# Opening transfers of a two-layer attention kernel: one key-half transfer on another queue, weight loads tied to a block of x, seven warming products

## The chip, the cores and the metric

The kernel runs on one core of a Trainium2 chip. Time is the device time of one execution in microseconds (us). The engines are PE (TensorE, matrix products; PEld is its weight load), DVE (VectorE), ACT (ScalarE), POOL (GpSimd) and SP (SyncE, which here only issues transfers). SP and ACT issue transfers on a queue of their own each (q1 and q10 in the profile), POOL on a third (q0). [...]

## The reference, cut to what matters

x has shape (4, 128, 64, 64): four images of 128 channels and n = 4096 tokens. All is f32.

```
# layer 0: attention over tokens, 64 media channels, no scale, no mask
xf  = x.reshape(b, c, n)
q, k, v = wq @ xf, wk @ xf, wv @ xf            # each (b, 64, n)
att = softmax(einsum('bmi,bmj->bij', k, q))
x   = x + wo @ einsum('bij,bmj->bmi', att, v)

# layer 1: tokens t = x as (b, n, 128)
t = t + causal_attention(layernorm(t), Wq, Wk, Wv)
t = t + ffn(layernorm(t), W, V, gamma, beta)   # W, batch norm over all tokens, then
                                               # y_t = sigmoid(wx_t + y_{t-1} @ V.T)
```

## The kernel before, in words

`kernel` builds two paths. `fast_path` computes the result and a flag; `general_path` follows only if the flag says that an assumption on the number ranges failed. All times here are of the fast path.

**Tiling.** A block is BLK = 512 tokens, an image has NB = 8 blocks and NT = 32 tiles of 128 tokens. `xs` holds all images in SBUF. Image 0 is loaded by SP in eight transfers of 256 KB, in the order of blocks 0, 4, 1, 5, 2, 6, 3, 7 (L424 to L426): the fifth block of x, number 4, is the second one loaded.

**Keys and queries of layer 0.** `cols0(b, m)` (L524) makes two products of 128x512: block m with `wqk` (queries in rows 0 to 63, keys in 64 to 127) and block m + 4 with `wkq` (the other way round). DVE copies the first result to `bt.kr`, ACT the second. The scores need queries and keys on the same partitions, so after each copy a transfer of 128 KB moves half of the rows to the other half of the partitions, into `bt.swap` (L541). The first of these transfers, b = 0, m = 0, h = 0, is read by the first score product. The one for h = 1 is read from query block 4 on (`rows0`, L575).

**Values of layer 0.** `vals0` (L543) makes the value product, ACT copies it, and for image 0 `vals0_by_tokens` (L569) turns it with four transposes.

**The opening.** L420 to L422 load `wqk`, `wkq` and `wv0` in five small transfers on ACT's queue. POOL makes `ident`. L457 to L460 load `wo2` (two halves), `wqT`, `wkT` and `wv1` on POOL's queue, and `load_rest` (L511), called once the side work of image 0 is done, issues four more there: `wf`, `vf`, `gamma`, `beta`. Nothing makes POOL wait before these nine, and all of them are issued within the first 7 us. TensorE first runs twelve 128x128 products of `ident` with itself (L494 to L496), whose results nobody reads; an f32 product appears as two records. Then L1008 sets the order of the first tasks:

```python
for task in parts[0][:2] + parts[1][:1] + parts[0][2:]:
    task()
```

So TensorE makes both key products of m = 0, the value product of m = 0, both key products of m = 1 and the four transposes, and then the loop of L1051 starts with the first `scores` (L883). The scratch results of all these (`misc`, L490) share two PSUM buffers, so each product waits until the result two before it is copied out.

**The loop.** Each step issues the scores of an item (two tiles of keys against one block of queries), then the values of the item two steps earlier, then the sums. One task of `side` or `waiting` is added where one is due: the remaining key and value products of image 0, then `form` (L506, reads `wqT` and `wkT`) and `form_half` (L498, reads `vf`, `beta` and `wf`).

The instructions of one engine are placed by a scheduler at build time, so an engine's order can differ from the order of the text where nothing forbids it: the issue of the first half of `wo2` stands ahead of the last step of `ident` on POOL.

Of the kernel before, what the change touches and what calls it, by code (L numbers as in the profile page):

```python
# [9 lines left out]
F32 = mybir.dt.float32  # L10
# [5 lines left out]
P = 128  # L16
BLK = 512
# [342 lines left out]
def fast_path(  # L360
# [22 lines left out]
    nc = tc.nc  # L383
    B, C, N = x.shape
    M = c_wqT.shape[1]
    assert C == P and M == P // 2 and N % CHUNK == 0
    NT = N // P
    NB = N // BLK
# [9 lines left out]
    const = ctx.enter_context(tc.tile_pool(name="const", bufs=1))  # L398
# [6 lines left out]
    xs = xpool.tile([P, B, N], F32, name="xs")  # L405
# [5 lines left out]
    def load(engine, name, shape, *parts):  # L411
        t = const.tile(shape, F32, name=name)
        for dst, src in parts:
            engine.dma_start(out=dst(t), in_=src)
        return t

    whole = lambda t: t
    lo, hi = (lambda t: t[:, 0:M]), (lambda t: t[:, M:P])
    top, bottom = (lambda t: t[0:M]), (lambda t: t[M:P])
# [29 lines left out]
    wf = const.tile([P, P], F32, name="wf")  # L449
    vf = const.tile([P, P], F32, name="vf")  # L450
# [3 lines left out]
    wfc = const.tile([P, P], F32, name="wfc")  # L454
    gamma = const.tile([P, 1], F32, name="gamma")
    beta = const.tile([P, 1], F32, name="beta")
    wo2 = load(nc.gpsimd, "wo2", [P, P], (top, c_woT), (bottom, c_woT))  # L457
    wqT = load(nc.gpsimd, "wqT", [P, P], (whole, a_wqT))
    wkT = load(nc.gpsimd, "wkT", [P, P], (whole, a_wkT))
    wv1 = load(nc.gpsimd, "wv1", [P, P], (whole, a_wv))  # L460
    good = const.tile([P, 2], F32, name="good")
    g1 = const.tile([P, P], F32, name="g1")
    recs = const.tile([P, 2, B, NT], F32, name="recs")
# [18 lines left out]
    with tc.tile_pool(name="batch", bufs=1) as batch, tc.tile_pool(name="rows", bufs=2) as rowp, tc.tile_pool(  # L482
        name="prob", bufs=4
    ) as prob, tc.tile_pool(name="work", bufs=2) as wk, tc.tile_pool(name="stat", bufs=4) as stat, tc.tile_pool(
        name="ps_s", bufs=2, space=PSUM
    ) as ps_s, tc.tile_pool(name="ps_a", bufs=1, space=PSUM) as ps_a, tc.tile_pool(
        name="ps_m", bufs=2, space=PSUM
    ) as ps_m:

        def misc(name):  # L490
            return ps_m.tile([P, BLK], F32, tag="m", name=name)


        wp = misc("warm_ps")  # L494
        for _ in range(12):
            nc.tensor.matmul(wp[:, :P], lhsT=ident, rhs=ident, start=True, stop=True)  # L496

        def form_half():  # L498
            hp = misc("h_ps")
            nc.tensor.matmul(hp[:, 0:1], lhsT=vf, rhs=point5, start=True, stop=True)  # L500
            nc.vector.tensor_tensor(beta_half, hp[:, 0:1], beta, ALU.add)
            cp = misc("c_ps")
            nc.tensor.matmul(cp[:, :P], lhsT=center, rhs=wf, start=True, stop=True)
            nc.vector.tensor_copy(wfc, cp[:, :P])

        def form():  # L506
            gp = misc("g_ps")
            nc.tensor.matmul(gp[:, :P], lhsT=wqT, rhs=wkT, start=True, stop=True)
            nc.vector.tensor_copy(g1, gp[:, :P])

        def load_rest():  # L511
            for t, src in ((wf, f_wT), (vf, f_vT), (gamma, f_gamma), (beta, f_beta)):
                nc.gpsimd.dma_start(out=t, in_=src)

        class Batch:
            pass
# [7 lines left out]
        def cols0(b, m):  # L524

            bt = bs[b]
            if m == 0:
                bt.kr = batch.tile([P, 2, N // 2], F32, tag="kr", name="kr")  # L530
                bt.swap = batch.tile([P, N // 2], F32, tag="swap", name="swap")
                bt.v = batch.tile([P, NT // 2, 2, M], F32, tag="v", name="v0")
            for h, w in enumerate((wqk, wkq)):
                ps = misc("kr_ps")
                nc.tensor.matmul(ps, lhsT=w, rhs=xs[:, b, ts(m + h * NB // 2, BLK)], start=True, stop=True)
                if h:
                    nc.scalar.copy(bt.kr[:, h, ts(m, BLK)], ps)
                else:
                    nc.vector.tensor_copy(bt.kr[:, h, ts(m, BLK)], ps)
                rows, keys = slice(M - h * M, P - h * M), slice(h * M, h * M + M)  # L540
                nc.sync.dma_start(out=bt.swap[keys, ts(m, BLK)], in_=bt.kr[rows, h, ts(m, BLK)])  # L541

        def vals0(b, m):  # L543

# [379 lines left out]
        def sums(it):  # L924

            if it.first:
                bs[it.b].dsum = wk.tile([P, 2, BLK], F32, tag="dsum", name="dsum")
            it.den = den = bs[it.b].dsum
            if all(n == BLK for _, _, n, _ in it.at):
                flat = den.rearrange("p a b -> p (a b)")  # L930
                if it.first:
                    nc.vector.tensor_copy(flat, it.p)  # L932
                else:
                    nc.vector.tensor_tensor(flat, flat, it.p, ALU.add)  # L934
                return
            for h, (t, q0, n, o) in enumerate(it.at):
                if it.first:
                    if q0:
                        nc.gpsimd.memset(den[:, h, :q0], 0.0)
                    nc.vector.tensor_copy(den[:, h, q0:], it.p[:, o : o + n])  # L940
                else:
                    nc.vector.tensor_tensor(den[:, h, q0:], den[:, h, q0:], it.p[:, o : o + n], ALU.add)  # L942
# [51 lines left out]
        def push(slot, chain):  # L994
            step = next(chain, None)
            if step:
                waiting.append((slot + step[0], step[1], chain))

        def keys(b, m):
            mem = []  # L1000
            return [
                lambda: cols0(b, m),
                lambda: mem.append(vals0(b, m)),
                lambda: b or vals0_by_tokens(b, m, mem[0]),
            ]
# [7 lines left out]
        def rows():  # L1013

            if blocks:
                layer, b, g = blocks.pop(0)
                (rows1 if layer else rows0)(b, g)
                if layer == 0:
                    started.append((b, g))

        def tokens():

            while started:
                b, g = started.pop(0)
                tokens0(b, g)
                if g == 2 and b + 1 < B:

                    nc.gpsimd.tensor_copy(
                        xs[:, b + 1].rearrange("p (k n) -> p k n", n=CHUNK)[:, :, 0], bs[b].agg[:, : N // CHUNK]
                    )  # L1030
                    for k in range(N // CHUNK):
                        nc.sync.dma_start(out=xs[:, b + 1, ts(k, CHUNK)], in_=x[b + 1, :, ts(k, CHUNK)])
# [6 lines left out]
        def begin(s):  # L1039
            nonlocal done  # L1040
            if done < s < len(items):
                done = s
                it = items[s]
                if it.first:
                    bs[it.b].rows = bs[it.b].next.pop(0)
                    if it.layer and it.g == 3 and it.b + 1 < B:
                        for m in range(NB // 2):
                            side.extend(keys(it.b + 1, m))
                scores(it)

        for s in range(len(items) + SKEW + 16):  # L1051
            begin(s)
            if SKEW < s < len(items) - 1 and items[s - SKEW].first and items[s + 1].layer == 0:
                ended = items[s - SKEW - 1]
                if ended.layer == 0 and ended.g not in visits[0]:
                    begin(s + 1)
            if 0 <= s - SKEW < len(items):
                it = items[s - SKEW]
                values(it)
                if it.last:  # L1060
                    rows()
                    tokens()
                    for k, g in enumerate(visits[it.layer].get(it.g, ())):
                        push(s, bs[it.b].leave[g](8 * k))
                    push(s, (finish1 if it.layer else finish0)(it.b, it.g))
            if s < len(items):
                sums(items[s])
            due = [w for w in waiting if w[0] <= s]
            if due:
                w = min(due, key=lambda w: w[0])  # L1070
                waiting.remove(w)
                w[1]()
                push(s, w[2])
            elif side:
                side.pop(0)()
                if not side and items[s].b == 0 and items[s].layer == 0:
                    tokens()
                    load_rest()
                    form_half()
        assert not waiting and not side  # L1080

# [5 lines left out]
    with tc.tile_pool(name="xr", bufs=1) as xrp, tc.tile_pool(name="y", bufs=2) as yp, tc.tile_pool(  # L1087
        name="sums", bufs=3
    ) as sums, tc.tile_pool(
        name="ps_y", bufs=1, space=PSUM  # L1090
# [3 lines left out]
        for b in range(BY_C):  # L1094
            for c in range(Q):
                nc.sync.dma_start(
                    out=xc[ts(c, S), b].rearrange("r (g k) s -> r g (k s)", g=NB),
                    in_=x2c[b, :, :, c].rearrange("g r n -> r g n"),
# [36 lines left out]
        late = xs.rearrange("p b (r h k q) -> p b k r h q", h=HALVES, r=TPB, q=P)  # L1135
# [149 lines left out]
```

## Time and profile before

| What | us |
|---|---|
| median of 3 runs (2053.29 to 2053.88) | 2053.53 |
| the profiled execution | 2054.28 |
| its span, first to last instruction | 2052.6 |
| TensorE busy in it | 2036.8 |
| issues of x on SP's queue, first and last start | 0.82, 6.80 |
| issues of weights on POOL's queue, first and last start | 1.43, 6.36 |
| first issue of a key-half transfer | 9.25 |
| first product of scores | 14.05 |
| product of `form`, first of `form_half` | 37.84, 38.17 |

The granted clock of TensorE was 0.999 over the span. In the profile's lines, `out<-in` gives the tiles that an instruction writes and reads, "x8" the number of instructions merged into the line, and the brackets at the end the idle time before it and what ended that. A line with q after the engine's name (SPq, ACTq, POOLq) is the issue of a transfer, or a wait of that engine's sequencer.

### The profile page before, as it was taken

Reading aid. Unit: us, or ns where it says so; the run is one execution under the profiler, and the core shown is the slowest. Engines: PE = TensorE matmul, PEld = TensorE weight load, DVE = VectorE, ACT = ScalarE, POOL = GpSimd, SP = SyncE. Lnnn points to the kernel's source line nnn. Section 1 sums busy time; section 2 is a strip of 40 time slices with the busy share of each in tenths; the row PEclk is TensorE's granted clock in tenths of the full one; section 3 lists DMA queues with packets and bytes.
Section 4 is the critical chain, followed back from the end, with each engine's and each line's share of the span. In section 5 each row is a group of like instructions: output and inputs, shape, how many; then the busy total and the mean of one; then the engine's idle time right before and its main releaser. Section 6 shows DMA issues by size and latency. Waiting matters only on the chain. (4 is left out here: it accounts for less than half of the span.)

```text
span 2052.6 us, 30794 instructions
## 1 busy us (share of the span) xinstructions
PE 2036.8 (99%) x11646; PEld 907.4 (44%) x11646; DVE 1486.6 (72%) x2862; ACT 989.1 (48%) x1071; POOL 137.5 (7%) x237
## 2 busy tenths in 40 slices
PE   9999999999999999999999999999999999999998
PEld 3643354444333345444433335444433334544456
DVE  4799877555889987555588997654578998765568
ACT  4666632323666653333466663333356665333346
POOL 1000011000000011000000001100000000100004
PEclk9999999999999999999999999999999999999999
DMA  3111021231201112222111001123000110210056
GB/s 88 53 33 27 12 42 37 51 79 37 58 2 23 22 22 42 47 62 67 22 53 22 17 17 42 37 68 82 16 17 2 22 23 12 52 42 21 21 115 225
DMA packets 237869, 89.03 MB, mean 43 GB/s; under 512 B 174752, under 2 KB 219296, under 8 KB 237200
## 3 DMA queue, kind: packets, MB, share of 16 engines
q1 hardware_dynamic: 236704, 86.42, 17.7%
q8 instruction: 93, 1.52, 0.3%
q14 instruction: 64, 0.52, 0.1%
q0 software_dynamic: 288, 0.39, 0.1%
q10 hardware_dynamic: 720, 0.16, 0.0%
HBM read 45.84 MB, written 36.89 MB: 40 GB/s over the span
## 5 line engine op out<-in xcount | busy, mean ns | idle before, releaser
L934 DVE TENSOR_TENSOR dsum<-dsum,p 128x1024 f32<-128x1024 f32 x676 | 826.1, 1222 | 429.6 <-ACT p L910 308.5
L908 ACT ACTIVATE p<-s_ps,nshift 128x1024 f32<-128x1024 f32 x512 | 569.3, 1116 | 318.4 <-PE s_ps L894 310.3
L910 ACT ACTIVATE p<-s_ps 128x1024 f32<-128x1024 f32 (+2 forms) x288 | 274.2, 952 | 609.5 <-PE s_ps L903 607.1
L954 PE MATMUL acc<-p,v 64*64 64x512 f32 x4096 | 543.0, 590 | 0.0
L894 PE MATMUL s_ps<-swap,kr 64*64 64x512 f32 x2048 | 539.0, 591 | 2.1 <-DMA swap<-kr 1.2
L894 PE MATMUL s_ps<-kr 64*64 64x512 f32 x2048 | 525.0, 591 | 0.0
L903 PE MATMUL s_ps<-rows,xhT 128*128 128x512 f32 (+3 forms) x1152 | 502.9, 559 | 0.0
L962 PE MATMUL acc<-p,xh 128*128 128x512 f32 (+3 forms) x1152 | 500.9, 557 | 0.0
L962 PEld LDWEIGHTS acc<-p,xh 128*128 128x128 f32 x1152 | 216.2, 190 | 244.3 <-issue 234.2
L903 PEld LDWEIGHTS s_ps<-rows,xhT 128*128 128x128 f32 x1152 | 214.0, 190 | 243.3 <-issue 203.4
L954 PEld LDWEIGHTS acc<-p,v 64*64 64x64 f32 x4096 | 166.6, 133 | 272.5 <-issue 251.6
L894 PEld LDWEIGHTS s_ps<-swap,kr 64*64 64x64 f32 x2048 | 151.4, 133 | 132.3 <-issue 107.7
L894 PEld LDWEIGHTS s_ps<-kr 64*64 64x64 f32 x2048 | 140.7, 133 | 138.0 <-issue 133.6
L666 POOL TENSOR_TENSOR ln_rstd<-ln_var,mhalf 128x4 f32<-128x4 f32 x64 | 68.2, 1065 | 1099.4 <-DVE ln_var L664 1099.4
L942 DVE TENSOR_TENSOR dsum<-dsum,p 128x256 f32<-128x256 f32 (+1 forms) x120 | 55.4, 497 | 64.3 <-POOL p L914 64.3
L652 DVE SCALAR_TENSOR_TENSOR xs<-o_ps,recs,xs 128x128 f32<-128x128 f32 x256 | 74.4, 341 | 3.1
L682 DVE TENSOR_SCALAR xh<-xs,ln_mv,ln_rstd 128x128 f32<-128x128 f32 x252 | 70.2, 342 | 2.2
L914 POOL TENSOR_SCALAR_AFFINE_SELECT p<-p 128x128 f32<-128x128 f32 x128 | 35.9, 304 | 486.4 <-ACT p L910 473.9
L661 DVE BATCH_NORM_STATS2 ln_st<-xs 128x6 f32<-128x128 f32 x256 | 63.2, 269 | 0.0
L932 DVE COPY dsum<-p 128x1024 f32<-128x1024 f32 x60 | 41.0, 683 | 16.0 <-ACT p L910 10.8
L839 ACT COPY xs<-wx_ps 128x512 f32<-128x512 f32 x31 | 18.1, 585 | 65.6 <-DVE stats L835 63.5
L1158 DVE SCALAR_TENSOR_TENSOR z<-xs,scale,y_ps 128x256 f32<-128x256 f32 x100 | 45.0, 480 | 2.6 <-PE y_ps L1156 1.6
(148 smaller groups left out, 989.6 us busy)
## 6 DMA issues: line engine op xcount, KB each, us to landing
xs<-in_xT SPq DMA_DIRECT2D x32, 256.0 KB, 3.0
by_r<-sqT SPq DMA_DIRECT2D x128, 64.0 KB, 2.2
xhT<-by_r SPq DMA_DIRECT2D x128, 64.0 KB, 2.0
by_c<-sqT SPq DMA_DIRECT2D x124, 64.0 KB, 1.8
xhT<-by_c SPq DMA_DIRECT2D x31, 256.0 KB, 2.7
xs<-in_x SPq DMA_DIRECT2D x12, 512.0 KB, 5.9
swap<-kr SPq DMA_DIRECT2D x32, 128.0 KB, 2.3
x2c<-sqT SPq DMA_DIRECT2D x64, 64.0 KB, 2.4
```

What stands on the lines that cost most here:

```text
L652: nc.vector.scalar_tensor_tensor(t, in0=op[:, ts(j, P)], scalar=rec[:, j : j + 1], in1=t, op0=ALU.mult, op1=ALU.add)
L661: nc.vector.bn_stats(st[:, j], xs[:, b, ds(g * BLK + j * P, P)])
L666: nc.gpsimd.tensor_tensor(y, var, mhalf, ALU.pow)
L682: nc.vector.tensor_scalar(dst[:, j], xs[:, b, ds(g * BLK + j * P, P)], mv[:, j, 0:1], y[:, j : j + 1], ALU.subtract, ALU.mult)
L894: nc.tensor.matmul(ps[c * M : c * M + M, off : off + n], lhsT=bs[it.b].kr[part, h, ds(t % (NT // 2) * P + c * M, M)], rhs=rows[h], start=True,
L903: nc.tensor.matmul(ps[:, off : off + n], lhsT=lhsT, rhs=rhs, start=True, stop=True)
L908: nc.scalar.activation(it.p[:, :off], ps[:, :off], AF.Exp, bias=nshift)
L910: nc.scalar.activation(it.p[:, :off], ps[:, :off], AF.Exp, scale=float(P) ** -0.5)
L934: nc.vector.tensor_tensor(flat, flat, it.p, ALU.add)
L942: nc.vector.tensor_tensor(den[:, h, q0:], den[:, h, q0:], it.p[:, o : o + n], ALU.add)
L954: nc.tensor.matmul(bt.acc[h * M : h * M + M, r], lhsT=bt.v[part, t % (NT // 2), t // (NT // 2)], rhs=it.p[part, o : o + n], start=it.first ...
L962: nc.tensor.matmul(bt.acc[:, 0, q0:], lhsT=bt.xh[:, t], rhs=it.p[:, o : o + n], start=it.first and h == 0, stop=it.last and h == 1,)
```

## The change

The nine weight loads of POOL are gathered in one place, before the loop. Ahead of each, POOL copies one column of block 4 of image 0 into the first column of the tile to be loaded, so the copy waits for that block, and the load, which overwrites the column, waits for the copy. The four loads of `load_rest` move there as well. The warming products become seven. The first of the key-half transfers is issued by ACT instead of SP.

```diff
-    wo2 = load(nc.gpsimd, "wo2", [P, P], (top, c_woT), (bottom, c_woT))
-    wqT = load(nc.gpsimd, "wqT", [P, P], (whole, a_wqT))
-    wkT = load(nc.gpsimd, "wkT", [P, P], (whole, a_wkT))
-    wv1 = load(nc.gpsimd, "wv1", [P, P], (whole, a_wv))
+    wo2 = const.tile([P, P], F32, name="wo2")
+    wqT = const.tile([P, P], F32, name="wqT")
+    wkT = const.tile([P, P], F32, name="wkT")
+    wv1 = const.tile([P, P], F32, name="wv1")
+
+    late = ((wqT, a_wqT), (wkT, a_wkT), (wo2[0:M], c_woT), (wo2[M:P], c_woT), (wv1, a_wv))
+    late += ((wf, f_wT), (vf, f_vT), (gamma, f_gamma), (beta, f_beta))
+    for t, src in late:
+        nc.gpsimd.tensor_copy(t[:, 0:1], xs[: t.shape[0], 0, (NB // 2) * BLK : (NB // 2) * BLK + 1])
+        nc.gpsimd.dma_start(out=t, in_=src)
...
         wp = misc("warm_ps")
-        for _ in range(12):
+        for _ in range(7):
             nc.tensor.matmul(wp[:, :P], lhsT=ident, rhs=ident, start=True, stop=True)
...
-        def load_rest():
-            for t, src in ((wf, f_wT), (vf, f_vT), (gamma, f_gamma), (beta, f_beta)):
-                nc.gpsimd.dma_start(out=t, in_=src)
...
-                nc.sync.dma_start(out=bt.swap[keys, ts(m, BLK)], in_=bt.kr[rows, h, ts(m, BLK)])
+
+                queue = nc.sync if b or m or h else nc.scalar
+                queue.dma_start(out=bt.swap[keys, ts(m, BLK)], in_=bt.kr[rows, h, ts(m, BLK)])
...
                     tokens()
-                    load_rest()
                     form_half()
```

## The prediction, made before the result was known

> **What bounds the kernel now.** I read the page first, then the waits of TensorE, then the first 15 us of the timeline, then the landing times of single transfers. The page:
>
> ```profile
> span 2052.6 us, 30794 instructions
> PE 2036.8 (99%) x11646; PEld 907.4 (44%) x11646; DVE 1486.6 (72%) x2862; ACT 989.1 (48%) x1071; POOL 137.5 (7%) x237
> ```
>
> TensorE is idle for 2052.6 - 2036.8 = 15.8 us in all. Its waits, over the whole span:
>
> ```profile
> PE warm_ps L496 <- POOL ident masks.py:199: 2.6, 1, 2.6
> PE s_ps L894 <- DMA swap<-kr: 1.2, 1, 1.2
> PE s_ps L894 <- ACT p L908: 0.9, 2, 0.5
> PE y_ps L1156 <- ACT y L1153: 0.8, 1, 0.8
> PE xh2T_ps L797 <- DVE xh L680: 0.8, 1, 0.8
> PE c_ps L503 <- DVE beta_half L501: 0.3, 1, 0.3
> PE wx_ps L828 <- DVE xhT L798: 0.3, 1, 0.3
> ```
>
> These make 6.9 us. The other 8.9 us lie after the last matmul (the timeline ends it near 2043.7). So from the first score product to the end TensorE hardly waits, and whatever brings the first score product forward moves everything behind it by as much. The question is only when that product starts. The timeline of the start:
>
> ```profile
> 0.82 6.31 SPq L426 DMA_DIRECT2D xs<-in_x  x8
> 1.43 0.71 POOL L414 DMA_DIRECT2D wo<-in_c_woT  x1 [0.31 <-issue]
> 2.25 0.30 POOL masks.py:199 TENSOR_SCALAR_AFFINE_SELECT ident<-ident 128x128 f32<-128x128 f32 x1
> 2.61 5.03 PE L496 MATMUL warm_ps<-ident 128*128 128x128 f32 x24 [2.61 <-POOL ident masks.py:199]
> 7.47 1.02 PE L535 MATMUL kr_ps<-xs,wqk 128*128 128x512 f32 x2
> 8.33 1.02 PE L535 MATMUL kr_ps<-xs,wkq 128*128 128x512 f32 x2
> 8.53 0.69 DVE L539 COPY kr<-kr_ps 128x512 f32<-128x512 f32 x1 [4.28 <-PE kr_ps L535]
> 9.28 1.08 PE L547 MATMUL v_ps<-xs,wv 128*64 128x512 f32 x4
> 9.39 0.58 ACT L537 COPY kr<-kr_ps 128x512 f32<-128x512 f32 x1 [4.91 <-PE kr_ps L535]
> 10.29 1.12 PE L535 MATMUL kr_ps<-xs,wqk 128*128 128x512 f32 x2
> 11.25 1.02 PE L535 MATMUL kr_ps<-xs,wkq 128*128 128x512 f32 x2
> 12.20 0.66 PE L572 MATMUL vT_ps<-ident,vT 128*128 128x128 f32 x4
> 14.05 0.65 PE L894 MATMUL s_ps<-swap,kr 64*64 64x512 f32 x2 [1.19 <-DMA swap<-kr]
> ```
>
> Columns are start, duration, engine, line. The reader should see three things. The warming products hold TensorE until 7.47. From there projections run back to back for 5.3 us, to about 12.8. Then TensorE waits for the first transfer of key halves and starts scoring at 14.05. By single landings (issue start plus time to landing, each asked of a narrow window): block 0 of x lands at 0.82 + 3.8 = 4.6, block 4 (the fifth, second in the order of loading) at 1.26 + 4.1 = 5.4, wqk's second half at 1.25 + 4.3 = 5.55, wkq's second half at 2.22 + 4.8 = 7.0, wv0 at 7.3, block 5 at 4.78 + 4.7 = 9.5, and the last two blocks near 12.9 and 13.6. The first swap is issued at 9.25 and takes 4.8, to 14.05; the ones issued from 12.17 on take 2.2 to 2.5. The page of that tile says the same:
>
> ```profile
> DMA to landing us min/median/max: 2.2/2.3/4.8
> ```
>
> **What the Trainium skill says.** "DMA: Bandwidth & Descriptors", section on queues, rings and completion order: SP and ACT each own one ring on each of the same 16 DMA engines, a ring is consumed in order, and an engine goes round robin between rings that have work. That fits: the swap on SP's ring took 4.8 behind four blocks of x, and 2.2 when nothing stood before it. "TensorE: Matmul & The Clock Gate", Part 1: the array starts at half clock and gets the full one after a busy window of about 3.4 us, and the windows run freely. The trace agrees in size: warming records start 0.213 us apart until about 7.0 and 0.11 apart after that, so full clock came 4.4 us after the first product at 2.61. Which share of a window must be busy, the page doesn't say.
>
> **The change, part by part.**
>
> Seven warming products. Five products are ten records fewer. Fourteen records at 0.213 take 3.0 us instead of 4.86. On POOL the load of wo2 (0.71) now stands ahead of the select that finishes ident; as that load moves away, I take ident to be ready about 0.7 earlier, so warming runs from about 1.9 to 4.9. If POOL's order leaves ident at 2.6, it ends at 5.6. Either way the first projection then waits for wqk: 5.55 before, and I take 5.5, since POOL's queue had moved only some 0.06 of its 0.39 MB by then. So it starts 2.0 earlier than at 7.47.
>
> But the clock is then still half. I keep full clock at 7.0. The first projection's two records need 0.86 at full clock; from 5.5 to 7.0 they do 0.75 of that, and 0.11 remains: it ends its issue at 7.1, not at 6.36, and its results are complete some 0.2 later (8.53 - 8.33 before). DVE's copy (0.69) ends at 8.0 instead of 9.22. The second projection needs wkq; POOL's traffic was dense at 5.5 to 6.5, so 7.0 should become about 6.4, and 7.1 holds anyway. From there the distances of before: 0.95 to the value product (8.05; it also needs the buffer that DVE frees at 8.0), 1.01 to the next key product (9.06), 0.96 (10.1), 0.95 (11.05), 0.60, first scores at 11.65.
>
> The swap on ACT's queue. The issue costs 0.45 on ACT (its rows at L414; SP's took 0.55), starting at 8.0 when DVE's copy is done. Queued behind it on ACT is the copy of the second key half: ready at 8.2, now started at 8.45, ended at 9.05; the third key product waits for this buffer, so it goes at 9.15 instead of 9.06. That is a cost of 0.1, put into the sum; for it TensorE waits and no one else. The landing takes between 2.2 (nothing beside it) and 4.8 (as on SP's ring). I take 2.9: 128 KB sharing the engines with x's ring. It lands at 10.9, before 11.7, with 0.8 to spare. The 1.2 us wait goes entirely; next late is TensorE's own string of projections. SP loses one issue, and its next swap (rows of the other half, used from block 4 on) is not urgent.
>
> The weights after block 4. Nine copies of 128x1 on POOL, about 0.12 each by the memset rows of that size, and the same nine issues at 0.54 to 0.71. From 5.4 they take some 7 us, last issue near 12, last landing at most 6.7 later: under 19. The first reader is g_ps (L508) at 37.84, about 35.4 when shifted; then beta_half; wo2 is read at 110. Cover of 16 us, so cost nothing. Block 5 is needed by the fourth key product at 10.1. Its landing at 9.5 gains from POOL's silence until 7 and loses afterwards to the weights and the swap; bounds 8.5 to 10.5, taken 9.4: not binding. If it were 10.5, 0.4 is lost.
>
> Sum: 14.05 - (11.65 + 0.1) = 2.3 us, all of it passing to the end. From its own execution, 2054.28 (span 2052.6 and 1.7 around it), 2052.0; the median of the runs shown is 0.75 lower, 2053.53, and I forecast from it: 2051.2. Unknown terms: ident earlier or not costs nothing unless it shifts the clock; a clock that rises at 6.0 gives 0.7 more; wqk's landing 0.3 either way; swap between 2.2 and 4.8 costs 0 to 1.0. The forecast's own range is 2050.2 to 2052.2.
>
> **The rivals.**
>
> *Late clock.* Warming ends at 4.9 and TensorE then idles until 5.5, so the window may not count as busy and the full clock comes one window later, 7.0 + 3.4 = 10.4. For it speaks that warming of 3.0 us is shorter than that window; against it that some 80% of the time up to 7.0 is still busy. 5.33 us of projection work from 5.5: 2.45 done at half clock by 10.4, 2.88 left, first scores at 13.3, gain 0.8: 2052.7.
>
> *Swap slow on ACT's ring* because the x blocks, the weights and it share the engines: 4.8 from 8.0 is 12.8, gain 1.25: 2052.3. The short landings after 12.17 speak against it, but x was done by then.
>
> *Slower.* Half clock lasts through the opening. Scores would start at 5.33 + (r + 5.5)/2 for full clock at r; this equals 14.05 at r = 11.9, from which point the change loses. At r = 14 it loses 1.0: 2054.5. A measurable loss of over 4.1 us needs half clock until about 20, or exposed waits of that size later, which the margins above don't show. Against: once the projections start, TensorE is busy without a gap, and before it took 4.4 us.
>
> *Faster than thought.* Full clock early and wkq at 6.0: scores at 10.4, gain 3.6: 2049.9. Block 5's landing forbids much more.
>
> **How the numbers follow.** Forecast 0.58, late clock 0.18, slow swap 0.07, faster than thought 0.06, slower than before 0.11. Predicted is the likeliest, 2051.2. The range takes the forecast, most of late clock and slow swap and the edge of faster: 2049.9 to 2053.3. The measurement can tell about 0.2%, 4.1 us, from no change; almost every case lies inside it. Faster by more than that needs scores before 9.95, which block 5 nearly excludes: 0.04, out of the last rival. Slower by more: 0.06, the longer half of the slower rival. Same: 0.90.
>
> **What would show it.** First scores at 11 to 12.3, with no wait for the swap; a projection's first pass lasting about 0.85 instead of 0.43; the swap landing in under 3.7 us; wkq before 6.8; g_ps and c_ps waiting for no weights; the tail after the last matmul as long as before. It is wrong if scores start after 13, if TensorE waits again for x or swap, or if new waits appear behind 40 us.

## The result, and the profile after

The changed kernel takes 2059.52 us (median of 8 executions, 2058.58 to 2060.14) against 2053.44 for the kernel before (8 executions, 2053.10 to 2053.88): ratio 1.003, 95% interval 1.0020 to 1.0039. It is 6.1 us slower, where 2.3 us less was forecast and 2053.3 us was the upper end of the range.

First the page of the changed kernel, and TensorE's waits over its span (us in total, times, longest):

```profile
span 2057.7 us, 30784 instructions
PE 2038.7 (99%) x11636; PEld 906.5 (44%) x11636; DVE 1486.9 (72%) x2862; ACT 989.5 (48%) x1071; POOL 137.1 (7%) x246
```

```profile
PE s_ps L898 <- DMA swap<-kr: 4.9, 1, 4.9
PE warm_ps L502 <- POOL ident masks.py:199: 1.6, 1, 1.6
PE s_ps L898 <- ACT p L912: 0.9, 2, 0.5
PE y_ps L1159 <- ACT y L1156: 0.8, 1, 0.8
PE xh2T_ps L801 <- DVE xh L684: 0.8, 1, 0.8
PE kr_ps L537 <- DMA wqk<-in_c_wkT: 0.7, 1, 0.7
PE c_ps L509 <- DVE g L515: 0.3, 1, 0.3
PE wx_ps L832 <- DVE xhT L802: 0.3, 1, 0.3
```

The wait for the first transfer of key halves was to go. It grew from 1.2 to 4.9 us. The wait of 0.7 us for `wqk` is new: the long warming had covered it. The other waits are as before or shorter, none of the nine late weights is waited for, and the last matmul ends 8.7 us before the end of the span as against 8.9. So the loss is made in the opening. Its timeline (start, duration, engine, line; L537 are the key products, L551 the value products, L576 the transposes, L898 the scores, L545 the key-half transfers):

```profile
1.57 3.36 PE L502 MATMUL warm_ps<-ident 128*128 128x128 f32 x14 [1.57 <-POOL ident masks.py:199]
5.59 1.10 PE L537 MATMUL kr_ps<-xs,wqk 128*128 128x512 f32 x2 [0.66 <-DMA wqk<-in_c_wkT]
6.55 1.10 PE L537 MATMUL kr_ps<-xs,wkq 128*128 128x512 f32 x2
7.45 0.52 ACTq L545 DMA_DIRECT2D swap<-kr  x1
7.58 1.08 PE L551 MATMUL v_ps<-xs,wv 128*64 128x512 f32 x4
7.99 1.28 ACT L539 ACT_TABLE_LOAD   x1 [7.99 <-DVE kr L541]
9.29 0.59 ACT L539 COPY kr<-kr_ps 128x512 f32<-128x512 f32 x1
13.59 1.97 PE L898 MATMUL s_ps<-swap,kr 64*64 64x512 f32 x2 [4.93 <-DMA swap<-kr]
15.49 2.07 PE L537 MATMUL kr_ps<-xs,wqk 128*128 128x512 f32 x2
17.35 1.59 PE L537 MATMUL kr_ps<-xs,wkq 128*128 128x512 f32 x2
18.78 0.60 PE L576 MATMUL vT_ps<-ident,vT 128*128 128x128 f32 x4
19.31 0.64 PE L898 MATMUL s_ps<-swap,kr 64*64 64x512 f32 x1
20.32 1.08 PE L551 MATMUL v_ps<-xs,wv 128*64 128x512 f32 x4
```

Three things differ from before. One product of the scores (two records) now stands **ahead** of the key products of m = 1 and the transposes. Those three need nothing from the transfer, yet in the trace they start only behind that product, at 15.49 and later, so they wait for the transfer too. The transfer, issued at 7.45, takes 6.1 us, to 13.55. And after the wait TensorE runs at half speed until about 18.5: a key product takes 1.9 us from start to start where it took 0.96. The sums of three stretches say the same (length, then busy time of PE, PEld, DVE, ACT, POOL, then the granted clock, DMA share and GB/s). The half clock begins within the wait, at about 11.7:

```profile
8.70:13.50 4.80, 0.00 (x0) 0.00 (x0) 0.00 (x0) 1.65 (x3) 2.43 (x6) 0.81 0.90 244
11.70:13.50 1.80, 0.00 (x0) 0.00 (x0) 0.00 (x0) 0.00 (x0) 0.02 (x1) 0.50 0.73 155
13.60:18.40 4.80, 4.80 (x6) 1.50 (x7) 0.69 (x1) 0.00 (x0) 0.42 (x1) 0.50 0.01 2
```

From there on the two kernels run alike: the value product of m = 1 starts at 20.32, before at 15.07, 5.25 later, and the spans differ by 5.1. (The medians differ by 6.1; the profiled execution of the kernel before, 2054.28, was one of its longer ones.) The 5.25 are: first score product 0.46 earlier (13.59 for 14.05); the two moved key products and the transposes, which took 2.5 us (10.29 to 12.8) under the transfer's flight and now come after it; half a clock over 4.8 us, 2.4; and 0.8 left over, in waits for PSUM buffers and copies among them.

### The profile page after: what moved, and what is told of

Its sections match the earlier page's. It is cut to its first block, busy times and chain, and to the rows that moved or that the text cites. A ratio compares the mean times of both kernels' runs of the same rounds, so it can differ in the third digit from the quotient of the medians.

```text
span 2057.7 us, 30784 instructions
## 1 busy us (share of the span) xinstructions
PE 2038.7 (99%) x11636; PEld 906.5 (44%) x11636; DVE 1486.9 (72%) x2862; ACT 989.5 (48%) x1071; POOL 137.1 (7%) x246
## 5 line engine op out<-in xcount | busy, mean ns | idle before, releaser
L898 PE MATMUL s_ps<-swap,kr 64*64 64x512 f32 x2048 | 540.9, 592 | 5.8 <-DMA swap<-kr 4.9
L898 PE MATMUL s_ps<-kr 64*64 64x512 f32 x2048 | 525.0, 591 | 0.0
L898 PEld LDWEIGHTS s_ps<-swap,kr 64*64 64x64 f32 x2048 | 151.7, 133 | 136.8 <-issue 107.9
L898 PEld LDWEIGHTS s_ps<-kr 64*64 64x64 f32 x2048 | 140.7, 133 | 138.0 <-issue 133.8
L936 DVE COPY dsum<-p 128x1024 f32<-128x1024 f32 x60 | 41.0, 683 | 15.1 <-ACT p L914 10.8
```

Of the source, the lines that this page charges most:

```text
L898: nc.tensor.matmul(ps[c * M : c * M + M, off : off + n], lhsT=bs[it.b].kr[part, h, ds(t % (NT // 2) * P + c * M, M)], rhs=rows[h], start=True,
```

## The experiments

Times are medians of 7 to 15 executions, each beside the kernel before on the same chip (2053.35, 2053.45 and 2053.36 us in the three groups). My theory after the result was ORDER: moving the transfer to ACT changed the order of TensorE at build time, and that made the loss. Rivals were the late weights, which share the DMA engines with the transfer (WEIGHTS), and the short warming (CLOCK).

**E1, the change without the moved transfer.**

```diff
-                queue = nc.sync if b or m or h else nc.scalar
-                queue.dma_start(
+                nc.sync.dma_start(
```

> The changed kernel with the first key-half transfer back on SP's queue; late weights and seven warming products stay. Theory ORDER (the transfer on ACT made the build place one score product ahead of the projections of m = 1, TensorE then stood 4.9 us and worked at half clock): the string of projections comes first again, first scores near 13, the time about 1 us below the kernel before, near 2052.4. Rival WEIGHTS (the late weights compete with the transfer) and rival CLOCK (seven warming products leave the array at half clock): still 4 to 6 us slower than before, near 2058.

2054.31 us, ratio 1.0006 (0.9998 to 1.0014). The order of before is back and all but 1 us of the loss is gone, but the gain of 1 us isn't there: the transfer, issued at 8.71, took 5.8 and landed at 14.5. In this execution the key products of m = 0 ran at half speed.

**E2, the kernel before with the moved transfer alone.**

```diff
-                nc.sync.dma_start(
+                queue = nc.sync if b or m or h else nc.scalar
+                queue.dma_start(
```

> The kernel before with nothing but the first key-half transfer moved to ACT's queue; twelve warming products, weights early. ORDER: slower than before by 4 to 6 us, 2057.5 to 2059.5, with one long wait of TensorE at the first score product and the projections of m = 1 behind it at half clock. WEIGHTS and CLOCK: within 1 us of before or up to 1 us faster, since neither part is in it.

2058.09 us, ratio 1.0022 (1.0014 to 1.0030): 4.7 us lost, with weights early and twelve warming products. Its timeline on TensorE shows the same order and the same half speed:

```profile
9.71 1.08 PE L549 MATMUL v_ps<-xs,wv 128*64 128x512 f32 x4
13.74 1.07 PE L896 MATMUL s_ps<-swap,kr 64*64 64x512 f32 x2 [2.95 <-DMA swap<-kr]
14.74 2.07 PE L535 MATMUL kr_ps<-xs,wqk 128*128 128x512 f32 x2
16.61 1.79 PE L535 MATMUL kr_ps<-xs,wkq 128*128 128x512 f32 x2
```

WEIGHTS and CLOCK fall as causes of this part of the loss; this one line makes most of the whole.

**E3, the whole change with the first item's scores pinned in TensorE's order.**

```diff
-                        nc.tensor.matmul(
+                        ins = nc.tensor.matmul(
...
+                        if it is items[0]:
+                            tc.keep_in_program_order(ins)
```

> The whole change, with the four products of the first score item pinned behind the projections in TensorE's order. ORDER: the loss goes, first scores near 13.6 when the transfer lands, 2052.5 to 2053.5. WEIGHTS and CLOCK: stays at 2057 or more, because the transfer still lands late and warming is still short.

2053.69 us, ratio 1.0003 (0.9995 to 1.0011). 5.8 us come back by the order alone, though the transfer is still slow (5.0); the time is a little above the 2052.5 to 2053.5 expected. The timeline shows what is next late:

```profile
7.82 0.52 ACTq L545 DMA_DIRECT2D swap<-kr  x1
8.37 1.28 ACT L539 ACT_TABLE_LOAD   x1 [8.37 <-DVE kr L541]
9.66 0.59 ACT L539 COPY kr<-kr_ps 128x512 f32<-128x512 f32 x1
10.30 1.13 PE L537 MATMUL kr_ps<-xs,wqk 128*128 128x512 f32 x2 [1.37 <-ACT kr L539]
12.85 0.65 PE L898 MATMUL s_ps<-swap,kr 64*64 64x512 f32 x2
```

In the kernel before, ACT loaded its table at 3.19, when it had nothing to do:

```profile
3.19 1.28 ACT L537 ACT_TABLE_LOAD   x1 [3.19 <-issue]
```

Now the transfer's issue stands ahead of it and waits for DVE, and table load and copy come after; TensorE's third key product waits 1.4 us for that copy.

**E4, the kernel before with seven warming products.**

```diff
-        for _ in range(12):
+        for _ in range(7):
```

> The kernel before with seven warming products and nothing else. ORDER: the projections start near 5.6, the transfer is issued near 7.6 but still lands when the blocks of x on its queue are done, 13.5 to 14, so the time is within 0.7 us of before. CLOCK: slower by 2 us or more.

2053.61 us, ratio 1.0002 (0.9994 to 1.0011). The projections start at 5.76 instead of 7.47, and nothing is won: the transfer is issued at 7.86 instead of 9.25 and lands at 13.95 instead of 14.05.

**E5, E3 with ACT's table loaded early.**

```diff
+    table = const.tile([P, 1], F32, name="table")
+    nc.scalar.copy(table, ones)
```

> The whole change, scores pinned, and a copy of one column on ACT early, so that ACT's table is loaded before ACT stands at the transfer. Theory TABLE (the waiting issue on ACT pushed the table load of 1.28 us, and with it the copy of the second key half, behind itself): TensorE's wait of 1.4 us for that copy goes, and since the transfer then lands no earlier, a wait of about 1 us for the transfer takes its place; the time is that of the pinned kernel or up to 0.5 us less. Rival (the copy was late for another reason): the 1.4 us wait stays.

2054.41 us, ratio 1.0005 (0.9996 to 1.0013). The 1.4 us wait for the copy is gone and the projections end at 10.9, but TensorE then waits 3.2 us for the transfer, which took 6.9 in this execution; a wait of 1 us was expected, and the time is 0.7 us above E3 instead of below it. Behind the wait the clock is at half again, from about 15.0 to 18.4 us:

```profile
14.10 0.65 PE L900 MATMUL s_ps<-swap,kr 64*64 64x512 f32 x2 [3.21 <-DMA swap<-kr]
15.15 1.97 PE L553 MATMUL v_ps<-xs,wv 128*64 128x512 f32 x4
15.10:18.30 3.20, 3.20 (x16) 0.60 (x12) 0.69 (x1) 1.70 (x2) 0.00 (x0) 0.50 0.02 5
```

TABLE was right about the copy, but its value is nothing as long as the transfer is late.

**E6, E3 with the weights early as before the change.**

> Seven warming products and the transfer on ACT, scores pinned, but the weights loaded early as before the change. Theory BACKLOG (the transfer waits for the blocks of x that were issued ahead of it, whichever queue it is on): its landing takes 4.5 to 5.5 us again, and the time is within 1 us of the pinned kernel. Rival WEIGHTS (late weights slow the transfer): landing under 4 us and 1 us faster than the pinned kernel.

2053.52 us, ratio 1.0001 (0.9992 to 1.0009), landing in 4.6. Beside E3, the late weights neither help nor harm while the transfer is late.

**E7, the last four blocks of x held back.** On the changed kernel, transfer on SP:

```diff
-    for m in range(NB // 2):
+    def load_x(m):
         for g in (m, m + NB // 2):
-            nc.sync.dma_start(out=xs[:, 0, ts(g, BLK)], in_=x[0, :, ts(g, BLK)])
+            tc.keep_in_program_order(nc.sync.dma_start(out=xs[:, 0, ts(g, BLK)], in_=x[0, :, ts(g, BLK)]))
+    load_x(0)
+    load_x(1)
...
+        parts[0][0]()
+        load_x(2)
+        load_x(3)
```

> Late weights, seven warming products, the transfer on SP, and the last four blocks of x issued behind the first two transfers of m = 0. BACKLOG: the first transfer lands 2.2 to 3 us after its issue, near 10.5, TensorE goes from the projections straight to the scores near 11.5, and the time is 2 to 3 us below before, 2050.4 to 2051.4. Rival (the transfer is slow under load for another reason): landing still over 4 us, time 2053 to 2054.

2051.31 us, ratio 0.9992 (0.9984 to 1.0000), 2.1 us below the kernel before in the medians, with an interval that just reaches no change. The transfer lands 3.1 us after its issue and TensorE goes into the scores without a wait:

```profile
7.49 1.33 SPq L547 DMA_DIRECT2D swap<-kr  x2
8.87 2.02 SPq L426 DMA_DIRECT2D xs<-in_x  x4
10.54 0.66 PE L578 MATMUL vT_ps<-ident,vT 128*128 128x128 f32 x4
11.13 0.65 PE L900 MATMUL s_ps<-swap,kr 64*64 64x512 f32 x2
```

**E8, the same with the transfer on ACT's queue**, scores pinned and table early.

> As the one with four blocks of x held back, but the transfer on ACT's queue, with ACT's table loaded early and the scores pinned. BACKLOG: landing 2.2 to 3 us here too and the same time as on SP within 0.7 us, so the queue itself is worth nothing. Rival QUEUE (ACT's queue is what helps): at least 1 us faster than on SP.

2051.77 us, ratio 0.9994 (0.9985 to 1.0002), landing in 2.7. The queue is worth nothing that these runs can tell.

**E9, the whole change with ACT's table loaded early, nothing pinned** (the two lines of E5 alone).

> The whole change, nothing pinned, and only the early copy of one column on ACT that brings the table load ahead of the waiting transfer issue. Theory TABLE-ORDER (it is the displaced table load that lets the build put a score product first: in its reckoning the second key half is copied so late that the score product looks ready sooner): the order of before comes back by itself and with it 2053 to 2055. Rival (the transfer on ACT alone changes the order): the 4.9 us wait and 2058 to 2060 stay.

2053.93 us, ratio 1.0004 (0.9995 to 1.0012). The order of before comes back by itself. So it isn't the queue as such but the table load that it pushed back; that this one early copy turns the order is shown. Why it does is not: the likely reason is that with the second key half copied later, the third key product, which needs that result's PSUM buffer, is reckoned to be ready later too, so that a score product is taken first. How the build reckons the times isn't in the trace. E9 shows one thing more: with TensorE's order of before and all three parts of the change, nothing is gained. The landing at 13.7 alone takes the forecast's 2.3 us.

**E10, the changed order with four blocks of x held back** (transfer on ACT, no pin, table not moved).

> The changed order of TensorE (one score product first, table load behind the transfer issue on ACT), but four blocks of x held back so that the transfer lands early. Theory PRODUCT (the order costs what the late landing makes of it): the transfer lands near 10, TensorE's wait is 1 to 2 us instead of 4.9, the array stays at full clock, 2051 to 2053. Rival (the order is bad in itself): 2056 or more.

2054.76 us, ratio 1.0005 (0.9997 to 1.0014). TensorE no longer waits for the transfer, but it lands at 11.0, not near 10, and neither 2051 to 2053 nor 2056 was met: the time is 3.0 us above E8. In the profiled execution full speed came only near 10.5: a pass of 512 columns takes 0.43 us at full speed (two of them 0.86 in the kernel before, 7.47 to 8.33), and those of the first key product take about twice that here.

```profile
5.49 2.05 PE L540 MATMUL kr_ps<-xs,wqk 128*128 128x512 f32 x2 [0.56 <-DMA wqk<-in_c_wkT]
9.18 1.73 PE L554 MATMUL v_ps<-xs,wv 128*64 128x512 f32 x4
11.03 1.07 PE L901 MATMUL s_ps<-swap,kr 64*64 64x512 f32 x2
5.50:10.40 4.90, 4.90 (x8) 1.44 (x8) 0.69 (x1) 1.54 (x2) 4.78 (x15) 1.00 0.41 130
```

The granted clock reads 1.00 in this stretch all the same: the half speed of the opening shows only in the lengths of the records, the half speed behind a wait shows in both. A rough estimate from the two profiled executions, 3.6 us apart (2054.76 and E8's 2051.18): 5 us at half speed are 2.5 us of work lost, in E8's opening some 0.2 are, which leaves about 1.3 us for the order. So most of the loss needs the late landing, but the order seems to cost something by itself; no run splits the two.

**E11, the whole change with twelve warming products.**

> The whole change with twelve warming products instead of seven. Theory ORDER: the wait for the transfer and the half clock behind it stay, 2058 to 2060. Rival CLOCK (the short warming makes the loss): 2055 or less.

2059.67 us, ratio 1.0029 (1.0018 to 1.0040). The projections of m = 0 run at full clock here from the first on, and it is as slow as with seven. CLOCK is out: the half clock comes with the wait, which is 4.8 us here.

**E12, E7 with twelve warming products.**

> Four blocks of x held back, transfer on SP, late weights, and twelve warming products: full clock before the projections in every execution. Theory PHASE (with seven products the executions fall into two groups 2 us apart by when the full clock comes): one group only, 2051.3 to 2052.3, spread under 1 us. Rival: the same two groups as with seven.

2052.11 us, ratio 0.9993 (0.9985 to 1.0002). The executions lie between 2051.5 and 2052.5. With seven products, E7 had eleven of thirteen at 2051.0 to 2052.0 and two at 2053.1 to 2053.6, E8 seven at 2050.9 to 2051.8 and six at 2053.2 to 2053.6. That fits a full clock that comes before the projections or some 4 us into them, since half speed over 4 us loses 2. The late case shows in profiles of other kernels (E1, E6, E10); the one profile of E7 and the one of E8 show the early case, so for these two it is not shown. With the transfer early, the shorter warming is worth about 0.8 us in the medians (2051.31 beside 2052.11): the first scores start at 11.13 in E7 and at 11.65 here.

**Landings of the first transfer**, from the single landing times of the profiles:

| kernel | queue | issued | took | landed |
|---|---|---|---|---|
| before | SP | 9.25 | 4.8 | 14.05 |
| after | ACT | 7.45 | 6.1 | 13.55 |
| E1 | SP | 8.71 | 5.8 | 14.5 |
| E2 | ACT | 9.69 | 4.0 | 13.7 |
| E3 | ACT | 7.82 | 5.0 | 12.8 |
| E4 | SP | 7.86 | 6.1 | 13.95 |
| E5 | ACT | 7.12 | 6.9 | 14.0 |
| E6 | ACT | 8.44 | 4.6 | 13.0 |
| E9 | ACT | 8.00 | 5.7 | 13.7 |
| E11 | ACT | 7.57 | 5.9 | 13.5 |
| E7, E12 (x held back) | SP | 7.49, 8.12 | 3.1, 2.4 | 10.6, 10.5 |
| E8, E10 (x held back) | ACT | 7.40, 8.30 | 2.7, 2.7 | 10.1, 11.0 |

With all eight blocks of x issued ahead, it lands at 12.8 to 14.5 whether issued at 7.1 or at 9.7, and on either queue. The three on SP's queue are late in that range (13.95 to 14.5; on ACT's 12.8 to 14.0), so ACT's queue may be worth some tenths; single executions don't tell. The packets of the changed kernel show what it waits for. First from the transfer's issue to 9.9, then from 9.9 to 13.6 (packets, MB, share of the 16 DMA engines; q1 is SP's queue, q10 ACT's, q0 POOL's):

```profile
q1 hardware_dynamic: 379, 0.68, 90.8%
q0 software_dynamic: 1, 0.00, 0.4%
```

```profile
q0 software_dynamic: 250, 0.39, 44.8%
q1 hardware_dynamic: 193, 0.33, 29.1%
q10 hardware_dynamic: 80, 0.13, 13.8%
```

For 2.4 us after its issue not one packet of ACT's queue moves, and POOL's weights, first issued at 6.65, move one. Only when most of x is through do the others begin, and then all at once. Part of the 2.4 us is there without x too: with x held back, the transfer's first packets moved about 1.2 us (E8) and 1.5 us (E7) after its issue.

## Why the prediction was wrong, point by point

- **The step that failed** is "From there the distances of before". It took TensorE's order of products as given: the third key product was to start at 9.15, ahead of all scores; it started at 15.49, behind a score product that waited for the transfer until 13.59. The front part says that the build may place an engine's instructions otherwise, and I had seen that the load of wo2 stood ahead of ident; I used this for POOL and not for TensorE. E2 makes 4.7 us of loss out of the moved transfer alone, E3 takes 5.8 back by the order alone.
- **Behind it, what stands behind the waiting issue on ACT.** I named one instruction, the copy of the second key half, and charged 0.1 us. There was a second: the table load of 1.28 us, which the timeline of before shows at 3.19, in the idle time that the issue now spends waiting. In the changed kernel the copy ends at 9.88, not 9.05. E3 shows it as 1.4 us of TensorE's time, E9 that it turned the order. The forecast's 0.1 us for the copy also seems to be counted twice: 9.06 + 0.96 is 10.0 and not 10.1, and the sum adds it again.
- **The landing** is a second step that failed, and it alone takes the gain (E9). It was to take 2.9 us, at most 4.8, on the argument that ACT's ring gets its turn beside SP's. It took 6.1, above my bound: the 4.8 was measured for an issue at 9.25, and issued 1.8 us earlier behind the same loads the transfer has longer to wait. The turn-taking between queues that the Trainium skill states ("DMA: Bandwidth & Descriptors", queues, rings and completion order) shows here only in part: in the kernel before, POOL's weights, issued from 1.43 on, moved 60 packets beside 309 of SP's queue from 7.0 to 9.5; in the changed kernel, with x issued ahead, ACT's queue moved none for 2.4 us, and with x held back SP's own queue was as good (E7, E8). What the prediction gives as agreement, 4.8 behind x and 2.2 without, bears on the order within SP's ring and not on turns between two. The rival of a slow swap named the mechanism; its 1.25 us of gain missed that the order would expose the whole of it.
- **The clock.** In the profiled execution the projections began at full clock, at 5.59, better than I took. The half clock came later, within the wait of 4.9 us. My slower rival had half clock as its cause; it is 2.4 of the 5.25 us, and from another source: E11 loses as much with twelve warming products. The rival fell short since it saw no wait to make it. (The rival of a faster start has a slip: with full clock from 5.5 on, 5.33 us of projections end at 10.8, not at 10.4.)
- **Right were:** the projections' start (5.5 forecast, 5.59), wkq before 6.8 (6.4), ident earlier (1.57), no wait for the nine late weights, the tail unchanged, all that happens in the opening passed on to the end. And seven warming products by themselves are worth nothing (E4), nor do the late weights change anything beside E6, as long as the transfer lands when it lands.
- **The 2.3 us exist.** E7 has them, 2.1 in the medians, by the way I had left out: fewer transfers ahead of the one that is waited for. Whether they need the late weights, which E7 keeps, no run shows.

## What to carry to other kernels

Where the build places an engine's instructions, a moved transfer can move matmuls: compare the order of every engine, not of the changed one alone, before pricing a step by the distances of the old trace. Before putting a waiting issue on an engine that computes, list everything that engine did in the idle time, table loads included. And in this kernel the transfer that is waited for came early by holding back the large ones ahead of it, not by another queue.

## What the runs showed of the hardware that I had not expected

- A transfer's landing hung on the loads issued ahead of it, on its own queue or another: ten landings at 12.8 to 14.5 us for issues spread over 2.6 us, and 2.4 to 3.1 us of flight once four blocks of x were behind it. By then the DMA engines had little else to do: in E7 their share was 0.02 from 7.0 to 7.5 us and 0.00 from 7.5 to 8.0.
- A wait can cost half the clock, and not only behind it. In the changed kernel and in E11 the granted clock was at 0.50 for 6.8 us, from about 11.7 and 11.4 on, within waits of 4.9 and 4.8 us; in E2, E5 and E9 for 3.4 us, from 14.7, 15.0 and 13.8 on, the first two about 1 us after waits of 2.9 and 3.2 us had ended. The length of the wait doesn't decide alone: in E9 2.0 us were enough, in E4 2.3 us were not. E9's stretch after its wait, then E4's:

```profile
13.70:17.30 3.60, 3.58 (x12) 0.57 (x12) 0.37 (x1) 1.11 (x1) 0.07 (x1) 0.53 0.12 34
13.96:17.36 3.40, 3.40 (x23) 0.96 (x24) 0.69 (x1) 1.80 (x3) 0.00 (x0) 1.00 0.02 8
```
